# Routing half of the tokens beside the last row's scans, with scatter transfers in turn

## The chip, the cores and the metric

The kernel runs on one core of a Trainium2 chip. Its time is the device time of one execution in microseconds. The core has a matrix engine (TensorE, PE in the profile; its weight loads are shown apart as PEld), three engines that work on 128-partition tiles (VectorE or DVE, ScalarE or ACT, GpSimd or POOL), and a queue that issues plain DMA transfers (SyncE or SP). Each engine executes its own instructions in the order of its program, and waits on semaphores for others.

## The reference

Four rows (B = 4) of 1024 tokens with D = 128 columns go through two layers. The first is a state-space layer, followed by a residual and a layer norm. The second is causal attention with a residual, then a mixture of experts, a residual and a last layer norm. Cut to what matters here:

```python
# layer 1: 256 inner channels, 16 states; h is a scan along the tokens
h = scan(dA, x_scaled);  y = einsum('bldn,bln->bld', h, Cp) + xb * D_param
x = layernorm(x + out_proj(layernorm(y) * silu(z)))
# layer 2
v = ln(x) @ v_w + v_b                       # q, k likewise; 16 heads of 8
hidden = x + (softmax(causal(q k^T)) v) @ o_w + o_b
xt = layer_norm(hidden).reshape(4096, 128)
logits = xt @ router_w                      # 16 experts
top1 = argmax(logits); top2 = argmax of the rest
loc1 = cumsum(m1) - 1;  loc2 = cumsum(m2) - 1 + m1.sum(0)   # m1, m2: one-hot choices
C = 512                                     # slots of an expert, later tokens are dropped
xin[e, slot] = xt[token];  eout = fc2(gelu(fc1(xin))) * 0.8
out = layernorm(x + hidden + g1 * eout[slot1] + g2 * eout[slot2])
```

A token's slot depends on how many tokens before it chose the same expert, so ranges of tokens must be routed in order. The reference puts second choices behind all first ones; the kernel counts second choices down from the end of an expert's slots instead, so it can place them before all first choices are known, and settles at the end which of them still have a slot.

## The kernel before

**Tiles and stages.** The 4096 tokens are 32 tiles of 128. `fronts` (L263) makes projections and the convolution of the four rows, and runs beside the scans of row 0. `scan_row` (in `scans`, L358) takes a row in two halves of 512 tokens. For each pair of state groups DVE multiplies (L529), scans (L539) and multiplies by C (L545), PE sums over states (L549). POOL copies the last states of the first half (`carry`, L542). `after_scans` (L458 to L520) normalises, and twice needs an inverse root on POOL (`pow`: `ssm_rs` in L152, `lnx_rs` in L518), for which DVE waits.

**Attention** (L644 to L972) runs beside the scans of the next row: `inputs` makes q, k and v of a half (k and q go through DRAM as three bf16 parts, `k_parts` and `q_parts`, and come back as `kst` and `qst`), adds v's bias on DVE (`vp`, L714), and a stream of score matmuls (L770), exponentials on ACT (`pr`, L780) and weighted sums (L792) follows. `rest_of_half` (L844) scales the sums (`avs`, L870), projects, adds o's bias, normalises, and writes tokens to DRAM (`x2_d`, and `rest_d` for the residual); L970 keeps the router's logits in `lg`. The last half has its own version, `group_of_last` (L880), which adds o's bias from a row in a matmul (`ob_row`).

**Routing.** `routing` (L1189) makes constants. `send(t0, n)` (L1241) routes n tiles: DVE finds the first choice (`top1`), PE counts tokens ahead of each one by triangular and all-ones matmuls (`places`, L1295 and L1298), DVE turns that into a slot (`to`, `put` in L1320), then the same for the second choice. For each tile and choice an indirect DMA on POOL (`scatter`, L126) writes 128 rows of 129 numbers (the token and its own number) into `xin`. Transfers of a range are declared to hit different rows, so those of a range don't wait for each other; the first waits for those of the range before. In the first range each waits for the range's first alone.

**The order.** `piece()` (L1519) takes the next steps of several queues of work: inputs (`before`), attention, the rest of halves (`after`), weight loads, routing (`aside`) and transfers (`sending`). PE's and DVE's orders are pinned as the program is written; ACT's, POOL's and SP's come from the tile scheduler. After row 3's scans a last loop runs what is left of the attention. `send_early` (L1609) starts there: the first range is 20 tiles (40 transfers), the second 8 (16 transfers), and the last 4 tiles (8 transfers) follow the loop. Then `experts` (L1405) runs the 16 experts and combines: it loads an expert's rows (L1420), two matmuls with a gelu between (L1434, L1435, L1441), scatters back to `eout`, reads both contributions of each token (`got`), and adds (L1486) `rest_d`, which was loaded into the 32 tiles of `xrow`.

Of the kernel before, what the change touches and what calls it, by code (L numbers as in the profile page):

```python
# [10 lines left out]
F32 = mybir.dt.float32  # L11
# [26 lines left out]
NFC = F // P  # L38
EARLY = 12
# [13 lines left out]
def mamba_then_moe_block_kernel(ctx: ExitStack, tc: tile.TileContext, a: dict, out: bass.AP):  # L53
# [304 lines left out]
    def scans(ph, pools, on_loads, on_scans, on_half, spare_bank=lambda: None):  # L358
# [5 lines left out]
        s3 = ph.enter_context(tc.tile_pool(name="scan3", bufs=3))  # L364
        s6 = ph.enter_context(tc.tile_pool(name="scan6", bufs=6))
# [3 lines left out]
        a_all = wts.tile([P, DI // NR, NS], F32, tag="a_all", name="a_all")  # L369
# [16 lines left out]
        a_own = wts.tile([P, DI // NR, NG_S, NI], F32, tag="a_own", name="a_own")  # L386
# [11 lines left out]
        def half_of_scans(b, hf):  # L398
# [5 lines left out]
            def spread_states(s, ts, name):  # L404
                t = s6.tile([P, HL], F32, tag=name, name=name)
                nc.sync.dma_start(t, bc_d[b][hf][s, len(ts)].unsqueeze(0).to_broadcast([NR, NI, HL]))
                ts.append(t)
# [200 lines left out]
    def attention_weights(wts):  # L608
# [20 lines left out]
        vb = load("vb", [P, D], a["v_b"].unsqueeze(0).partition_broadcast(P), wts)  # L629
# [3 lines left out]
        wo = load("wo", [P, NG, D], a["o_w_pad"].rearrange("g p e -> p g e"), wts)  # L633
        identb = wts.tile([P, P], BF16, tag="identb", name="identb")
# [7 lines left out]
        return wq, wk, qb, kb, wv, wo, wr, vb, ob, sel_b, identb, mask_k  # L642

    def attention(ph, weights, last_bank):  # L644
# [3 lines left out]
        wq, wk, qb, kb, wv, wo, wr, vb, ob, sel_b, identb, mask_k = weights  # L648
# [7 lines left out]
        def inputs(b, hf, x1, norm, made):  # L656
# [30 lines left out]
            for n, w, bias in (("q", wq, qb), ("k", wk, kb)):  # L687
# [26 lines left out]
            nc.vector.tensor_tensor(  # L714
                vp[:, :, 0 : H * (HD + 1)].rearrange("p i (h d) -> p i h d", d=HD + 1)[:, :, :, 0:HD],
                pv.rearrange("p (i h d) -> p i h d", h=H, d=HD),
                vb.rearrange("p (h d) -> p h d", d=HD).unsqueeze(1).to_broadcast([P, 4, H, HD]), ALU.add,
# [122 lines left out]

        ob_row = load("ob_row", [1, D], a["o_b"].unsqueeze(0), p1)
# [38 lines left out]
        def group_of_last(e, g, t, rows, i0, n):  # L880
# [10 lines left out]
            if g == 0:  # L891
                e.sel = p1.tile([P, NG, 32], F32, tag="xnT", name="sel_sum")
                nc.vector.tensor_copy(
                    e.sel, ident.rearrange("p (j r) -> p j r", r=32)[:, :, HD : HD + 1].to_broadcast([P, NG, 32])
                )
                e.po = last_bank("po")
                nc.tensor.matmul(
                    e.po, lhsT=one_row, rhs=ob_row.unsqueeze(1).to_broadcast([1, TPH, D]), start=True, stop=False
                )
# [32 lines left out]
        def after_projection(e, pt, rows, i0, n, hid=None):  # L932
# [15 lines left out]
            else:  # L948
                to = rows.xrow[:, t0 : t0 + n, 0:D]
# [239 lines left out]
    def routing(ph, bank):  # L1189
# [6 lines left out]
        keep = ph.enter_context(tc.tile_pool(name="rt_keep", bufs=1))  # L1196

# [6 lines left out]
        tri_f = load("tri", [P, P], a["c_tri"], keep)  # L1204
        tri = keep.tile([P, P], BF16, tag="tri_b", name="tri_b")
        nc.vector.tensor_copy(tri, tri_f)
        ones = keep.tile([P, P], BF16, tag="ones", name="ones")
        nc.vector.memset(ones, 1.0)
        iota_i = keep.tile([P, E], I32, tag="iota_i", name="iota_i")
        nc.gpsimd.iota(iota_i, pattern=[[1, E]], base=-E, channel_multiplier=0)  # L1210
        iota_e = keep.tile([P, E], F32, tag="iota_e", name="iota_e")
        nc.vector.tensor_copy(iota_e, iota_i)
        token_i = keep.tile([P, NT], I32, tag="token_i", name="token_i")
        nc.gpsimd.iota(token_i, pattern=[[P, NT]], base=0, channel_multiplier=1)
        token = per_token("token")
        nc.vector.tensor_copy(token, token_i)
        xrow = keep.tile([P, NT, D + 1], F32, tag="xrow", name="xrow")
        nc.vector.tensor_copy(xrow[:, :, D], token)
        second = keep.tile([P, NT, E], BF16, tag="second", name="second")

        first_slot = [E * CAP - 1, E * CAP + CAP]
        alt = [per_token(f"alt{i}") for i in range(2)]
        for i in range(2):
            nc.vector.tensor_scalar(alt[i], token, float(NSLOT + i * T - first_slot[i]), None, ALU.add)
        at2, p2, place2 = per_token("at2"), per_token("p2"), per_token("place2")
        put = [keep.tile([P, NT], I32, tag=f"put{i}", name=f"put{i}") for i in range(2)]
        totals, sent = [None, None], []
        behind = keep.tile([P, E, CAP // P], F32, tag="behind", name="behind")

        def has_slot(t0, n):  # L1230

            ts = slice(t0, t0 + n)
            full = p1.tile([P, n, E], F32, tag="full", name="full")
            tt(full, second[:, ts, :], totals[0].unsqueeze(1).to_broadcast([P, n, E]), ALU.mult)
            ok = p1.tile([P, n], F32, tag="ok2", name="ok2")
            nc.vector.tensor_reduce(ok, full, AX.X, ALU.add)
            tt(ok, ok, place2[:, ts], ALU.add)
# [3 lines left out]
        def send(t0, n, later=None):  # L1241
# [3 lines left out]
            def full(name):  # L1245
                return p1.tile([P, n, E], F32, tag=name, name=name)
# [7 lines left out]
            iota_b = iota_e.unsqueeze(1).to_broadcast([P, n, E])  # L1254

            group = (f"sent{t0}", [])
            earlier = sent[-1] if sent else []
            sent.append(group[1])

            def transfers(i):  # L1260
                for t in range(t0, t0 + n):
                    ins = scatter(xin, put[i][:, t : t + 1], xrow[:, t, :], group, earlier)
                    if len(group[1]) == 1 or earlier:
                        wait_for(ins, earlier)
                    yield

            def send_rows(i):
# [3 lines left out]
                else:  # L1271
                    later(transfers(i))

# [10 lines left out]
            def places(m, i, name):  # L1284
# [5 lines left out]
                mms = [(pcum, tri, mf)]  # L1290
                mms += [(pcum[:, t * E :], ones, mf[:, 0 : (n - t) * E]) for t in range(1, n)]
# [5 lines left out]
                for t in range(n):  # L1297
                    nc.tensor.matmul(ptot, lhsT=ones, rhs=m[:, t, :], start=(t == 0), stop=(t == n - 1))  # L1298
                yield USE
                tt(loc, pcum.rearrange("p (t e) -> p t e", e=E), m, ALU.mult)  # L1300
# [10 lines left out]
            def to(i, at, place, ok):  # L1311
# [5 lines left out]
                tt(slot, slot, alt[i][:, ts], ALU.subtract)  # L1317
                tt(slot, slot, ok, ALU.mult)
                tt(slot, slot, alt[i][:, ts], ALU.add)
                nc.vector.tensor_scalar(put[i][:, ts], slot, float(first_slot[i]), None, ALU.add)  # L1320

            loc = full("loc")
# [8 lines left out]
            place1 = yield from places(m1, 0, "place1")  # L1331
# [7 lines left out]
            lg2 = full("lg2")  # L1339
            nc.vector.scalar_tensor_tensor(lg2, m1, -BIG, x, ALU.mult, ALU.add)  # L1340
            m2 = second[:, ts, :]
            mx2 = top1(lg2, m2, at2[:, ts], "mx2")
            yield
            place = yield from places(m2, 1, "place")
            nc.vector.tensor_scalar(place2[:, ts], place, -1.0, None, ALU.add)
            ok2 = has_slot(t0, n)
            to(1, at2[:, ts], place, ok2)
            send_rows(1)
            nc.vector.tensor_reduce(z, pr, AX.X, ALU.add)
            nc.vector.reciprocal(z, z)  # L1350
# [4 lines left out]
            tt(p2[:, ts], mx2, z, ALU.mult)  # L1355
            tt(gates[1][:, ts], p2[:, ts], ok2, ALU.mult)

            if later is None:
# [6 lines left out]
                    behind, pos.unsqueeze(1).to_broadcast([P, E, CAP // P]),  # L1365
                    totals[0].unsqueeze(2).to_broadcast([P, E, CAP // P]), ALU.is_ge,
                )
                nc.vector.tensor_scalar(behind, behind, float(T), None, ALU.mult)
        def all_sent(early):

            if early:
                tt(gates[1][:, 0:early], p2[:, 0:early], has_slot(0, early), ALU.mult)
# [8 lines left out]
        return xrow, send, all_sent, (behind, sent), tri_f  # L1381
# [346 lines left out]
```

## Time and profile before

| | us |
|---|---|
| runs, median of 3 | 1277.84 (1274.19 to 1285.11) |
| the profiled execution | 1291.07 |
| its span on the core | 1289.3 |
| PE busy | 937.8 (73%) |
| DVE busy | 879.9 (68%) |
| ACT busy | 673.6 (52%) |
| POOL busy | 240.3 (19%) |
| transfers into `xin`, 64 (L126) | 61.8, 965 ns each |
| mean TensorE clock granted | 0.822 of full |

The page divides the span into 40 slices of 32.2 us; each digit is an engine's busy share of a slice in tenths. Row 0 with `fronts` takes up to some 240 us, the scans of rows 1 to 3 up to about 860, the rest of the attention up to about 1100, the experts up to 1255, and the combination the rest. A timeline line has the start, the duration, the engine, the line and operation, out<-in, shapes, a count, and in brackets the idle time before it and what ended it. A waits line has who waited for whom, the total, the number of times and the longest. "remote" or "issue" there means that nothing that the profile shows released the instruction.

### The profile page before, as it was taken

How to read it: one execution, taken by the hardware profiler on the slowest of the kernel's cores; microseconds unless marked ns; L12 is line 12 of the kernel's file. 1: busy time of each engine (PE TensorE's matmuls, PEld its weight loads, DVE VectorE, ACT ScalarE, POOL GpSimd, SP SyncE). 2: the span in 40 equal slices, each digit the busy share in tenths (PEclk: the TensorE clock that was granted, in tenths of full speed). 3: DMA queues.
4: the chain of work that ended last, by engine and by line, in shares of the span. 5: the costliest groups of instructions: out<-in, count | busy, mean ns of one | idle time of the engine just before them, and what ended most of it. 6: DMA issues, size and time to landing. Idle time of an engine off the chain costs nothing. (4 is left out here: it accounts for less than half of the span.)

```text
span 1289.3 us, 15308 instructions
## 1 busy us (share of the span) xinstructions
PE 937.8 (73%) x5376; PEld 445.8 (35%) x5376; DVE 879.9 (68%) x1298; ACT 673.6 (52%) x996; POOL 240.3 (19%) x231
## 2 busy tenths in 40 slices
PE   4677851368899986889985789976428684589965
PEld 2232310035433343234332333343102232456655
DVE  2199698998999999998999998975313346122115
ACT  1467556234777784676863486834214251733324
POOL 0020111032002002012012012000650401234443
PEclk9898976567989898898987698987657696789997
DMA  3965576536535535533543440464413100712117
GB/s 71 338 218 180 183 262 224 172 98 185 180 123 185 159 110 174 155 103 120 173 134 108 142 132 10 135 146 127 139 38 101 52 11 15 203 45 66 58 35 197
DMA packets 168329, 171.02 MB, mean 133 GB/s; under 512 B 31553, under 2 KB 123154, under 8 KB 168114
## 3 DMA queue, kind: packets, MB, share of 16 engines
q1 hardware_dynamic: 152418, 142.90, 36.4%
q10 hardware_dynamic: 11728, 18.62, 4.0%
q0 software_dynamic: 4096, 8.43, 2.0%
q8 instruction: 44, 0.72, 0.2%
q14 instruction: 43, 0.35, 0.1%
HBM read 110.80 MB, written 59.10 MB: 132 GB/s over the span
## 5 line engine op out<-in xcount | busy, mean ns | idle before, releaser
L780 ACT ACTIVATE pr<-pst 128x1024 f32<-128x1024 f32 (+3 forms) x396 | 293.0, 792 | 170.2 <-PE pst L770 66.8
L533 ACT ACTIVATE da<-dt_sp,a_neg 128x512 f32<-128x512 f32 x256 | 178.7, 723 | 113.0 <-DVE h L539 101.1
L770 PE MATMUL pst<-qst,kst 72*128 72x512 bf16 (+3 forms) x792 | 199.2, 353 | 50.6 <-ACT pr L780 32.7
L792 PE MATMUL av<-pr,vp 128*32 128x512 f32 (+3 forms) x1584 | 186.9, 542 | 2.4 <-DVE pr L783 1.9
L529 DVE TENSOR_TENSOR h<-u_sp,bt 128x2048 f32<-128x2048 f32 x64 | 145.3, 2274 | 17.1 <-DMA sz_d<-sz 17.1
L539 DVE TENSOR_TENSOR_SCAN h<-da,carry,h 128x512 f32<-128x512 f32 x128 | 155.7, 1264 | 1.7 <-ACT da L533 1.7
L539 DVE TENSOR_TENSOR_SCAN h<-da,h 128x512 f32<-128x512 f32 x128 | 148.3, 1205 | 6.8 <-ACT da L533 6.8
L549 PE MATMUL py<-h,sel 128*32 128x512 f32 x512 | 87.3, 761 | 83.0 <-DVE h L545 53.5
L545 DVE TENSOR_TENSOR h<-h,ct 128x2048 f32<-128x2048 f32 x64 | 146.1, 2283 | 1.1 <-POOL carry L542 0.3
L770 PEld LDWEIGHTS <-kst 72*128 72x128 bf16 x792 | 66.2, 103 | 231.5 <-issue 211.7
L542 POOL COPY carry<-h 128x4 f32<-128x4 f32 x32 | 42.0, 1313 | 372.0 <-DVE h L539 353.3
L126 POOL DMA_INDIRECT xin<-xrow,put x64 | 61.8, 965 | 166.8 <-DVE put L1320 81.8
L1435 ACT ACTIVATE hT<-ph,b 128x512 f32<-128x512 f32 x64 | 43.8, 687 | 81.0 <-PE ph L1434 80.3
L126 POOL DMA_INDIRECT eout<-eo,to x64 | 61.3, 957 | 92.4 <-DVE eo L1446 55.4
L300 PE MATMUL pt_x<-xT,w_tap 128*128 128x512 f32 x128 | 62.8, 649 | 16.8 <-DMA xT<-in_xT_dram 7.5
L1434 PE MATMUL ph<-xeT,w 128*128 128x512 f32 x128 | 63.6, 634 | 14.8 <-DVE xeT L1430 14.8
L1441 PEld LDWEIGHTS po_e<-w,hT 128*128 128x128 f32 x512 | 61.6, 192 | 12.9 <-issue 12.0
L1441 PE MATMUL po_e<-w,hT 128*128 128x128 f32 x512 | 63.3, 276 | 0.1
L776 PE MATMUL pst<-mask_k,identb 128*128 128x128 bf16 x448 | 62.7, 224 | 0.0
L792 PEld LDWEIGHTS av<-pr,vp 128*32 128x32 f32 x1584 | 37.1, 114 | 62.4 <-issue 39.0
L549 PEld LDWEIGHTS py<-h,sel 128*32 128x32 f32 x512 | 12.5, 120 | 125.3 <-DVE h L545 65.1
L776 PEld LDWEIGHTS <-identb 128*128 128x128 bf16 x448 | 43.0, 101 | 25.7 <-issue 5.8
(247 smaller groups left out, 1148.4 us busy)
## 6 DMA issues: line engine op xcount, KB each, us to landing
dt_sp<-dt_d SPq DMA_DIRECT2D x64, 256.0 KB
u_sp<-u_d SPq DMA_DIRECT2D x64, 256.0 KB
kst<-k_parts SPq DMA_DIRECT2D x96, 144.0 KB
qst<-q_parts SPq DMA_DIRECT2D x64, 144.0 KB
bt<-bc_d SPq DMA_DIRECT2D x32, 256.0 KB
ct<-bc_d SPq DMA_DIRECT2D x32, 256.0 KB
w<-in_fc_w_dram SPq DMA_DIRECT2D x32, 256.0 KB
xin<-clear SPq DMA_DIRECT2D x8, 516.0 KB
```

The source lines that it names most:

```text
L126: ins = nc.gpsimd.indirect_dma_start(out=dst[:, :], out_offset=bass.IndirectOffsetOnAxis(ap=rows, axis=0), in_=src, in_offset=None).ins
L529: nc.vector.tensor_tensor(s.h, s.u, four(s.bt), ALU.mult)
L533: nc.scalar.activation(s.da[jl], s.dt[:, jl, :], AF.Exp, scale=a_neg[:, j, s.g : s.g + 1])
L539: ins = nc.vector.tensor_tensor_scan(h, s.da[jl], h, from_, ALU.mult, ALU.add).ins
L545: nc.vector.tensor_tensor(s.h, s.h, four(s.ct), ALU.mult)
L549: nc.tensor.matmul(s.py[jl * NR : (jl + 1) * NR, :], lhsT=sel, rhs=s.h[:, jl, :], start=(s.g == 0), stop=(s.g == NG_S - 1),)
L770: nc.tensor.matmul(pst[:, jj, :w], lhsT=ks[ki // TPH][jp][:, jj, ki % TPH * P : (ki % TPH + 1) * P], rhs=qs[jp][:, jj, q0:c1], start=True, ...
L776: nc.tensor.matmul(pst[:, jj, :P], lhsT=identb, rhs=mask_k, start=False, stop=True)
L780: nc.scalar.activation(pr[:, :, :w], pst[:, :, :w], AF.Exp, scale=QSCALE)
L792: nc.tensor.matmul(av[32 * j : 32 * j + 32, q0 : q0 + w], lhsT=e.vps[ki // TPH][:, ki % TPH, v0 : v0 + 32], rhs=pr[:, jj, :w], start=(ki = ...
L1434: nc.tensor.matmul(phh, lhsT=w1[e][:, c * P : (c + 1) * P], rhs=xeT, start=True, stop=True)
L1441: nc.tensor.matmul(po[:, i, :], lhsT=hT[:, c, i * P : (i + 1) * P], rhs=w2[e][:, c, :], start=(c == 0), stop=(c == NFC - 1),)
```

## The change

Six things change.

1. `SOON` = 16 tiles (rows 0 and 1) are a range of their own. When the fourth half is finished, during row 3's scans, `send(0, 16, ..., staged=True)` joins the queue `after`. Its transfers go out by `both_transfers`: for each tile the row is read again from `x2_d` (64 KB, SP) into one of two buffers, POOL copies the token's number in, and then both choices' transfers follow, each a step of `piece()`. The constants move to row 0 (`begin`).
2. Transfers of all ranges but the last are in turn: each waits until the one before has landed. The last range's wait for the last of those, and not for each other.
3. The tail's ranges are 8, 4 and the last 4 tiles. `xrow` has 16 tiles.
4. v's bias isn't added to v: since the weights of a token sum to one, it adds v_b @ o_w to the projection. The setup adds that to `ob`; `vp` becomes a copy on ACT, and `ob_row` with a one-row matmul becomes `ob_diag`, a diagonal matrix under an all-ones matmul.
5. Buffers: 5 instead of 6 for `bt` and `ct`, 4 instead of 5 for `got`; `a_all` and `a_own` lie in a buffer of `h`; several wide tiles of the routing share one; the residual of the first 16 tiles is loaded into its own tile (`left`).
6. The slot arithmetic of `to` takes the token and a scalar in one operation where it had a tile `alt`, and `all_sent` works in two pieces.

```diff
+SOON = 2 * TPB
...
+        once = s3.tile([P, NJ, HL], F32, tag="h", name="a_once")
+        a_all = once[:, 0, 0 : DI // NR * NS].rearrange("p (m s) -> p m s", s=NS)
...
-                t = s6.tile([P, HL], F32, tag=name, name=name)
+                t = s5.tile([P, HL], F32, tag=name, name=name)
...
+        vb = wts.tile([P, NG], F32, tag="vb", name="vb")
+        nc.gpsimd.memset(vb, 0.0)
+        for j in range(H // NG):
+            nc.sync.dma_start(
+                vb[32 * j : 32 * j + HD, :], a["v_b"].rearrange("(g j d) -> j d g", g=NG, d=HD)[j]
+            )
+        pb = bank("pb_v")
+        for g in range(NG):
+            nc.tensor.matmul(pb[:, 0:1], lhsT=wo[:, g, :], rhs=vb[:, g : g + 1], start=(g == 0), stop=(g == NG - 1))
+        nc.vector.tensor_tensor(ob, ob, pb[:, 0:1], ALU.add)
...
-            nc.vector.tensor_tensor(
+            nc.scalar.copy(
                 vp[:, :, 0 : H * (HD + 1)].rearrange("p i (h d) -> p i h d", d=HD + 1)[:, :, :, 0:HD],
                 pv.rearrange("p (i h d) -> p i h d", h=H, d=HD),
-                vb.rearrange("p (h d) -> p h d", d=HD).unsqueeze(1).to_broadcast([P, 4, H, HD]), ALU.add,
             )
...
-                    e.po, lhsT=one_row, rhs=ob_row.unsqueeze(1).to_broadcast([1, TPH, D]), start=True, stop=False
+                    e.po, lhsT=rows.ones, rhs=rows.ob_diag.unsqueeze(1).to_broadcast([P, TPH, D]), start=True, stop=False
...
-        def send(t0, n, later=None):
+        def send(t0, n, bank, later=None, staged=False):
...
-            group = (f"sent{t0}", [])
-            earlier = sent[-1] if sent else []
-            sent.append(group[1])
+            group = (f"sent{t0}", []) if later is None else None
+            earlier = in_turn[-1:]
+            if group:
+                sent.append(group[1])
+
+            def transfer(i, t, row):
+                ins = scatter(xin, s.put[i][:, t : t + 1], row, group, earlier)
+                if group:
+                    wait_for(ins, earlier)
+                else:
+                    in_turn[:] = [ins]
...
+            def both_transfers():
+
+                for t in range(t0, t0 + n):
+                    row = p2.tile([P, D + 1], F32, tag="row", name="row")
+                    nc.sync.dma_start(row[:, 0:D], x2_d[t * P : (t + 1) * P, :])
+                    nc.gpsimd.tensor_copy(row[:, D : D + 1], s.token[:, t : t + 1])
+                    yield
+                    for i in range(2):
+                        yield
+                        transfer(i, t, row)
+                        yield
...
-                tt(slot, slot, alt[i][:, ts], ALU.subtract)
+                nc.vector.scalar_tensor_tensor(slot, slot, -alt[i], s.token[:, ts], ALU.add, ALU.subtract)
                 tt(slot, slot, ok, ALU.mult)
-                tt(slot, slot, alt[i][:, ts], ALU.add)
-                nc.vector.tensor_scalar(put[i][:, ts], slot, float(first_slot[i]), None, ALU.add)
+                nc.vector.scalar_tensor_tensor(
+                    s.put[i][:, ts], slot, alt[i] + first_slot[i], s.token[:, ts], ALU.add, ALU.add
+                )
...
-        p5 = ph.enter_context(tc.tile_pool(name="moe5", bufs=5))
+        p5 = ph.enter_context(tc.tile_pool(name="moe5", bufs=4))
...
-                nc.sync.dma_start(xrow[:, :, 0:D], rest_d.rearrange("(i p) d -> p i d", p=P))
+                rest = [(xrow[:, :, 0:D], row0, NT)]
+                if row0:
+                    rest.append((p6.tile([P, row0, D], F32, tag="left", name="left"), 0, row0))
+                for t, i, j in rest:
+                    nc.sync.dma_start(t, rest_d[i * P : j * P, :].rearrange("(i p) d -> p i d", p=P))
...
-                read = (nc.scalar if k and t0 < 20 else nc.sync).dma_start(
+                read = (nc.scalar if k and t0 < 16 else nc.sync).dma_start(
...
-                                if s is aside and before or (s is loads or s is sending) and (before or middle and not pace.block):
+                                late_one = s is loads or s is sending
+                                if pace.first and ((s is aside or late_one) and before or late_one and middle and not pace.block):
                                     continue
...
                     finished.append(rest)
+                    if len(finished) * TPH == SOON:
+                        after.append(send(0, SOON, bank_z, sending.append, staged=True))
...
-                        if not aside and early < len(finished) * TPH < NT and (not early or len(finished) > 2 * B - 2):
-                            aside.append(send_early(early, len(finished) * TPH - early))
-                            early = len(finished) * TPH
+                        known = len(finished) * TPH
+                        if not aside and not before and early < known < NT and (early == SOON or known > NT - 2 * TPH):
+                            aside.append(send_early(early, known - early))
+                            early = known
                         piece()
```

## The prediction

> **What bounds the kernel now.** I read the page's slices first, then busy time by windows, then the timelines and the waits of the window that stood out.
>
> ```profile
> PE   4677851368899986889985789976428684589965
> DVE  2199698998999999998999998975313346122115
> POOL 0020111032002002012012012000650401234443
> ```
>
> One digit is 32.2 us. VectorE is at 8 or 9 from slice 7 to slice 26, so rows' scans (240 to 860 us) are bound by DVE: what is added to DVE there is paid in full. From 860 us PE leads, except in slices 28 to 30 (903 to 967 us), where no engine is busy but POOL. By windows (PE, PEld, DVE, ACT, POOL busy with instruction counts, PE clock, DMA share, GB/s):
>
> ```profile
> 780.00:840.00 60.00, 54.61 (x408) 24.10 (x406) 52.93 (x66) 45.64 (x68) 6.59 (x2) 0.97 0.25 79
> 870.00:900.00 30.00, 20.06 (x113) 10.02 (x112) 16.60 (x57) 13.18 (x20) 1.64 (x1) 0.77 0.39 118
> 930.00:960.00 30.00, 4.00 (x13) 0.69 (x13) 1.72 (x5) 2.15 (x3) 20.33 (x22) 0.50 0.15 48
> 960.00:990.00 30.00, 22.95 (x89) 8.24 (x88) 10.27 (x39) 11.72 (x16) 0.00 (x0) 0.67 0.27 81
> ```
>
> In 930 to 960 PE has 4 us of work where its neighbours have 20 to 23. It isn't bandwidth: DMA is at 0.15. What fills this window is POOL's row of transfers into `xin` (L126), 40 of them with nothing between (start, duration, then the idle time before the instruction):
>
> ```profile
> 904.79 1.20 POOL L126 DMA_INDIRECT xin<-xrow,put  x1 [32.99 <-DVE put L1320]
> 907.81 0.96 POOL L126 DMA_INDIRECT xin<-xrow,put  x1 [1.82 <-DMA xin<-xrow,put]
> 909.08 0.96 POOL L126 DMA_INDIRECT xin<-xrow,put  x1 [0.30 <-issue]
> ...
> 955.78 0.96 POOL L126 DMA_INDIRECT xin<-xrow,put  x1 [0.30 <-issue]
> ```
>
> PE in the same time:
>
> ```profile
> 916.37 1.03 PE L770 MATMUL pst<-qst,kst 72*128 72x512 bf16 x2 [4.49 <-issue]
> 933.56 0.58 PE L868 MATMUL pr<-ih,sel_b 48*128 48x512 bf16 x1 [13.10 <-DVE avs L870]
> 937.33 0.80 PE L770 MATMUL pst<-qst,kst 72*128 72x384 bf16 x2 [2.43 <-ACT pr L780]
> 961.45 0.58 PE L868 MATMUL pr<-ih,sel_b 48*128 48x512 bf16 x1 [21.45 <-DVE avs L870]
> ```
>
> 4.49 + 13.10 + 2.43 + 21.45 = 41.5 us idle, and the last gap ends 5 us after the last transfer. The engines named as releasers were waiting too:
>
> ```profile
> DVE avs L870 <- remote: 23.0, 1, 23.0
> ACT pr L780 <- remote: 22.1, 3, 15.3
> ```
>
> "remote" means that no instruction the profile shows released them: DVE's L870 had its matmul (933.56, 0.58 us) done at 934.1, was free at 937.7, and started at 960.7. In the raw events PE's semaphore rises within about 1 us of the start of the matmul that signals it in other stretches, but with a median of 4.4 us and up to 10 us late in 910 to 940, and later still after that. So what stalls PE, DVE and ACT is that PE's completions arrive late while transfers go out back to back. The second burst (16, 1005.6 to 1025.7 us) shows it smaller: PE gaps of 4.00, 1.14 and 5.25 us. Bursts of four (expert outputs) show updates at most about 1.6 us late, with one exception. The lateness grows with the length of the burst.
>
> **What the Trainium skill says.** Perfetto Trace Analysis, "DMA Instruction — SWDGE (GPSIMD)": the time shown for such a transfer is that of writing its descriptors, not of moving data. DMA: Bandwidth & Descriptors, "Anatomy of one DMA — SWDGE (gpsimd) path": about 2.0 us fixed cost, mostly the receipt of the last write. The trace agrees: the first transfer lands 2.3 to 2.7 us after its issue, and the next, which waits for it, issues at +3.02 us. So a transfer in turn costs 3.02 us, against 1.26 in a burst. SBUF — State Buffer, "Who interferes with whom": a DVE instruction with two SBUF inputs and a GpSimd one that reads SBUF exclude each other for a whole instruction. The trace agrees for ordinary POOL work:
>
> ```profile
> 732.52 0.19 POOL L542 COPY carry<-h 128x4 f32<-128x4 f32 x1 [11.95 <-DVE h L539]
> 755.90 2.17 POOL L542 COPY carry<-h 128x4 f32<-128x4 f32 x1 [7.60 <-DVE h L539]
> 788.73 2.98 POOL L152 TENSOR_TENSOR ssm_rs<-ssm_ve,neg_half 128x4 f32<-128x4 f32 x1 [30.66 <-DVE ssm_ve L150]
> 864.76 1.01 POOL L152 TENSOR_TENSOR ssm_rs<-ssm_ve,neg_half 128x4 f32<-128x4 f32 x1 [9.13 <-DVE ssm_ve L150]
> ```
>
> The same copy takes 0.19 us, or 2.17 when it starts just after a 2.26 us multiply (L529, 755.76). For transfers the trace speaks against it: in the second burst the cadence stays 1.26 to 1.27 us although L783 and L1199, with two SBUF inputs, run across transfers' starts (`full`, 1010.65 to 1010.93, over the one at 1010.87), and DVE's own starts don't slip. No page bears on PE's late semaphore.
>
> **The change part by part**, against the profiled execution (1291.07 us, of which 1289.3 span and 1.8 around it). It is 13.2 above the median of the runs, 1277.84; I take the same difference off the median, which assumes that the stalls are as long without the profiler.
>
> 1. The burst of 40 leaves the tail. 32 of its transfers go beside row 3's scans, in turn. Removed: 41.5 us of PE gaps, less some 1.5 us that PE idles in 8 us of such work anyway: -40.
> 2. The ranges left in the tail are 8 and 4 tiles, in turn (16 × 3.02 = 48 us and 8 × 3.02 = 24 us of POOL, both over well before about 1045, when the last range isn't known yet; no `pow` of POOL is in the tail). Removed: 10.4 us less about 2.4 usual idling: -8. What in-turn transfers still delay is shown only by one: the transfer at 904.79, beside which PE ran on without a gap. Bounds for 24 of them: 0, and 24 × 0.55 (the second burst's loss per transfer, 8.8 / 16) = 13. I take +3.
> 3. Routing matmuls in PE's chain: the 20-tile range has 2 × (1 + 19 + 20) of them; the first set took 907.56 to 909.5, about 2 us. A range of 8 costs about 1.1 (1007.82 to 1008.9), so 2 × 0.9, and the third range, 4 for 8, less again; with DVE's shorter operations (0.49 us at 128x320, 0.29 at 128x128) that PE's last attention steps queue behind: -4 in all (0 to -6).
> 4. Routing of 16 tiles beside the scans, on DVE: 19 wide operations; 128x256 isn't in the trace, between 0.49 and 0.29 gives 0.42, so 8.0; 20 narrow ones at 0.2, 4.0. Sum +12.0. Seven of eight `vp` adds (L714) leave DVE during scans: 0.68 us busy, next start after about 0.6, -4.2. They become copies on ACT, busy 45.6 of 60 us in 780 to 840, so hidden; if ACT were full there, they would cost 8 × about 0.7. The constants at 853.3 to 854.2 move to the setup, -1. Net +7, all on the bound engine.
> 5. POOL's and SP's queues. POOL's order after: eleven transfers stand ahead of `ssm_rs` of half (3,0), two more ahead of `lnx_rs`, all 32 ahead of the last `ssm_rs`; DVE stops for each `pow` at once (0.90 and 1.53 us at 791.7 and 798.5). First slots (`put0`) are ready at about 759, second ones at about 770 by DVE's new order. With a cadence c the eleventh transfer is out at 770 + 9c + 1, the 32nd at 770 + 30c + 1; the `pow`s are due at about 799 and, since 864.8 + 7 is when the last `ssm_ve` comes, 872. At c = 3.02 these are 798 and 862: in time. The tiny row copies and carry copies run in the 1.8 us between a transfer's end and its landing; one held by a 2.27 us multiply can overrun that by half a microsecond. At c = 3.2 to 3.3, 1 to 2 us are lost at the first `pow` and as much at the next; +4. Each row's load on SP waits for the transfers of two rows before, with `sums`, the `q_parts` stores and `kst`/`qst` loads behind it; that is the same lag, not a second one, up to 2 us of it ahead of the `kst` loads near 822. DMA is at 0.25 there: 16 × 64 KB more is nothing. Bounds: 0, and 20 at c = 4.0 (a 1 us lock wait at each transfer: 770 + 120 + 1 - 872 = 19).
> 6. The rest: bias columns and four matmuls of one column in the setup, 5 instead of 6 `bt`/`ct` buffers, the 1 MB of `left` ahead of the first expert's rows and 4 instead of 5 `got` buffers: -4 to +6, I take +2. `ob_diag` makes a 1-row matmul a 128-row one of the same columns: 0.
>
> Sum: -40 - 8 + 3 - 4 + 7 + 4 + 2 = -36. Profiled 1255; median 1277.8 - 36 = 1242.
>
> **The rivals.**
> - The stall mostly stays, or is partly the profiler's: in-turn transfers too make PE's completions late (+13 instead of +3 in part 2 and as much again in row 3), or the 13 us by which the profiled execution is longer are stall that the timed runs lack. Either gives -36 + 10 to + 25: 1252 to 1267. For it: nothing tells why bursts do this. Against: no gap beside the single transfer, and the growth with burst length.
> - Slower: POOL's in-order queue holds the `pow`s, and so DVE, behind transfers. The loss is 30c - 101; without it the sum is -40, so the change turns harmful from c = 4.7 us. If descriptors are written only between DVE's instructions, or landings come late behind 256 KB loads, c = 5.5 gives +64: 1277.8 - 40 + 64 = 1302. For it: POOL's `pow` at three times its time beside scans. Against: the uniform cadence beside L783 and L1199, and the landing wait (1.8 us) that absorbs part of each delay.
> - Between: c = 4.0, +20 instead of +4: 1258.
> - The scheduler's order could fail to send during the scans; the instruction order of the built kernel excludes it.
>
> **How the numbers follow.** Forecast (1227 to 1253) 0.62; better, under 1227, 0.05; c about 4 or a partial stall (1253 to 1276) 0.20; slower 0.13. From 1226 to 1276 all but about 2 in 10 is held. One per cent, 12.8 us, is what a measurement of this kernel can tell from no change: faster 0.79, same 0.09, slower 0.12.
>
> **What would show it.** Right: slices 28 to 30 at PE's 6 to 7, no "remote" wait of over 3 us on DVE L870's and ACT L780's successors, transfers 3.0 us apart between 759 and 870, the last row's scans ending about 7 to 12 us later. Wrong: DVE waiting long on POOL's `ssm_rs` and `lnx_rs` in row 3, transfers over 4 us apart there, or PE gaps in the tail beside transfers in turn.

## The result

The changed kernel takes 1238.95 us (median of 4 runs, 1231.83 to 1255.13); the kernel before, run beside it, 1281.47. The ratio is 0.965, 95% interval 0.9554 to 0.9747: 3.5% faster, where the forecast was 1242. Medians here are over all runs, but ratios leave out slow ones: of the changed kernel the run of 1255.13, over 1.5% above its fastest. The profiled execution is the one of 1231.83 us, with a span of 1229.9.

Slices of the page (one digit is 30.7 us):

```profile
PE   4687852267889888889988497987878873789965
DVE  2199698999899999899999999788543555112205
POOL 1020012130211001101102213454103202244443
```

The hole is gone: PE has 8, 7 and 8 in slices 28 to 30 (the first slice is 0). In the kernel before it lay in slices 28 and 29, with 4 and 2. POOL has new work in slices 24 to 27, beside row 3's scans. By windows (PE, PEld, DVE, ACT, POOL busy with counts, PE clock, DMA share, GB/s):

```profile
760.00:840.00 80.00, 64.24 (x408) 25.48 (x400) 67.60 (x70) 51.34 (x74) 39.67 (x35) 0.82 0.29 86
930.00:960.00 30.00, 25.41 (x96) 9.22 (x100) 8.43 (x34) 10.63 (x14) 9.79 (x11) 0.70 0.32 96
960.00:990.00 30.00, 25.77 (x190) 9.88 (x191) 19.57 (x58) 19.05 (x29) 7.30 (x8) 1.00 0.16 48
```

PE is busy 25 of 30 us from 930 to 960, against 4 before, with eleven transfers beside it. POOL's timeline:

```profile
755.74 0.97 POOL L127 DMA_INDIRECT xin<-row,put  x1 [8.01 <-DVE mx L1211]
...
824.07 4.06 POOL L127 DMA_INDIRECT xin<-row,put  x1 [3.37 <-issue]
...
864.09 0.96 POOL L127 DMA_INDIRECT xin<-row,put  x1 [2.65 <-issue]
869.97 0.96 POOL L127 DMA_INDIRECT xin<-row,put  x1 [4.92 <-DMA xin<-row,put]
871.36 1.05 POOL L153 TENSOR_TENSOR ssm_rs<-ssm_ve,neg_half 128x4 f32<-128x4 f32 x1 [0.43 <-DVE ssm_ve L151]
...
941.53 0.96 POOL L127 DMA_INDIRECT xin<-xrow,put  x1 [1.58 <-DMA xin<-xrow,put]
...
1036.59 0.96 POOL L127 DMA_INDIRECT xin<-xrow,put  x1 [45.30 <-DVE p L1211]
```

In the tail, after row 3's scans, most transfers start 2.55 us or little more after the one before. Beside the scans it is slower: 29 steps from 755.74 to 864.09 are 3.74 us each, and one transfer took 4.06 us of POOL instead of 0.96. The last `ssm_rs` still starts when its input is there (0.43 us on DVE, not on a transfer).

Between the two profiled executions 59.4 us went: the last `ssm_rs` is at 871.4 instead of 864.8 (+6.6); from there to the first transfer of the last range it is 165.2 us instead of 225.8 (-60.6); from there to the end 193.3 instead of 198.7 (-5.4). Row 3 alone takes 19.5 us longer, 191.8 instead of 172.3; the changed execution was 12.9 us ahead when that row began, which nothing here explains.

### The profile page after: what moved, and what is told of

Read it like the earlier page. It is cut to its first block, busy times and chain, and to the rows that moved or that the text cites. A ratio compares the mean times of both kernels' runs of the same rounds, so it can differ in the third digit from the quotient of the medians.

```text
span 1229.9 us, 15466 instructions
## 1 busy us (share of the span) xinstructions
PE 923.8 (75%) x5388; PEld 442.2 (36%) x5388; DVE 880.8 (72%) x1328; ACT 678.4 (55%) x1006; POOL 265.2 (22%) x248
## 5 line engine op out<-in xcount | busy, mean ns | idle before, releaser
L536 ACT ACTIVATE da<-dt_sp,a_neg 128x512 f32<-128x512 f32 x256 | 179.0, 722 | 117.9 <-DVE h L542 106.8
L804 PE MATMUL av<-pr,vp 128*32 128x512 f32 (+3 forms) x1584 | 181.3, 526 | 2.0 <-DVE pr L795 1.6
L532 DVE TENSOR_TENSOR h<-u_sp,bt 128x2048 f32<-128x2048 f32 x64 | 145.4, 2276 | 16.5 <-DMA u_sp<-u_d 16.5
L782 PEld LDWEIGHTS <-kst 72*128 72x128 bf16 x792 | 66.3, 103 | 183.0 <-issue 153.5
L545 POOL COPY carry<-h 128x4 f32<-128x4 f32 x32 | 44.6, 1392 | 355.6 <-DVE h L542 336.9
L1476 PE MATMUL ph<-xeT,w 128*128 128x512 f32 x128 | 61.9, 619 | 12.9 <-DVE xeT L1472 12.9
L127 POOL DMA_INDIRECT xin<-row,put x32 | 47.0, 1468 | 77.1 <-issue 29.3
L127 POOL DMA_INDIRECT xin<-xrow,put x32 | 31.1, 971 | 137.5 <-DVE p L1211 45.3
```

The costliest lines, as they stand in the source:

```text
L127: ins = nc.gpsimd.indirect_dma_start(out=dst[:, :], out_offset=bass.IndirectOffsetOnAxis(ap=rows, axis=0), in_=src, in_offset=None).ins
L532: nc.vector.tensor_tensor(s.h, s.u, four(s.bt), ALU.mult)
L536: nc.scalar.activation(s.da[jl], s.dt[:, jl, :], AF.Exp, scale=a_neg[:, j, s.g : s.g + 1])
L782: nc.tensor.matmul(pst[:, jj, :w], lhsT=ks[ki // TPH][jp][:, jj, ki % TPH * P : (ki % TPH + 1) * P], rhs=qs[jp][:, jj, q0:c1], start=True, ...
L804: nc.tensor.matmul(av[32 * j : 32 * j + 32, q0 : q0 + w], lhsT=e.vps[ki // TPH][:, ki % TPH, v0 : v0 + 32], rhs=pr[:, jj, :w], start=(ki = ...
L1476: nc.tensor.matmul(phh, lhsT=w1[e][:, c * P : (c + 1) * P], rhs=xeT, start=True, stop=True)
```

## The experiments

They were run in sets, each on one chip with runs of the kernel before beside it; ratios are to those. The theory (T): transfers sent back to back make completions reach the engines late, and the gain comes from ending that. The rival (P, place): it comes from moving routing and transfers out of the tail.

| set, kernel before | kernel | median us | ratio (95% interval) |
|---|---|---|---|
| first, 1281.47 | the changed kernel | 1238.95 | 0.965 (0.9554 to 0.9747) |
| second, 1284.1 | before_turn | 1268.66 | 0.9881 (0.9854 to 0.9907) |
| | before_two | 1242.27 | 0.9702 (0.9629 to 0.9774) |
| | before_spaced | 1271.32 | 0.9912 (0.988 to 0.9944) |
| | after_tail_burst | 1256.8 | 0.9795 (0.9762 to 0.9827) |
| third, 1283.15 | after_soon0 | 1272.58 | 0.9907 (0.9877 to 0.9936) |
| | after_v_on_dve | 1247.84 | 0.969 (0.9637 to 0.9742) |
| | after_two | 1243.9 | 0.962 (0.9552 to 0.9688) |
| | soon0_two | 1246.63 | 0.9699 (0.9647 to 0.975) |
| fourth, 1231.7 | after_again | 1247.51 | 1.0108 (1.006 to 1.0155) |
| | after_last_two | 1239.74 | 1.0091 (1.0062 to 1.0119) |
| | spaced_write | 1238.79 | 1.0059 (1.0038 to 1.0079) |
| fifth, 1282.59 | soon0_burst | 1281.37 | 0.9985 (0.9963 to 1.0007) |

### Transfers in turn alone

```diff
-            group = (f"sent{t0}", [])
-            earlier = sent[-1] if sent else []
-            sent.append(group[1])
+            group = (f"sent{t0}", []) if later is None else None
+            earlier = in_turn[-1:]
+            if group:
+                sent.append(group[1])
...
-                    if len(group[1]) == 1 or earlier:
-                        wait_for(ins, earlier)
+                    if group:
+                        wait_for(ins, earlier)
+                    else:
+                        in_turn[:] = [ins]
```

> The kernel before with one edit: the transfers of the first two ranges (40 and 16) wait each for the landing of the one before; routing and transfers stay in the tail. Theory (transfers sent back to back make the semaphores of all engines late): the PE gaps beside the first two ranges go, 42 + 8 us, a little of it given back since POOL needs 102 us for 40 transfers, so 35 to 50 us faster than before (ratio 0.962 to 0.973). Rival (the gain of the change comes from moving routing and transfers out of the tail): within 1% of before.

Only 15 us faster, neither of the two. The gaps did go: windows, PE's timeline and waits of before_turn:

```profile
930.00:960.00 30.00, 26.45 (x149) 9.83 (x142) 14.08 (x45) 11.50 (x17) 9.57 (x10) 0.73 0.24 70
```

```profile
1027.60 0.27 PE L1301 MATMUL pcum<-second,ones 128*128 128x16 bf16 x4
1079.63 1.11 PE L1431 MATMUL pt_xe<-ident,xe 128*128 128x128 f32 x4 [51.75 <-DMA xe<-xin]
```

```profile
POOL xin L126 <- DMA xin<-xrow,put: 111.6, 56, 4.7
DVE to_f L1426 <- DMA xe<-xin: 57.9, 6, 47.2
```

PE ends the attention at 1027.6, some 60 us before it did. From the last `ssm_rs` to the end of the last routing matmul, in the kernel before, in before_turn and in the changed kernel:

```profile
864.76:1091.21 226.45, 135.80 (x819) 58.10 (x817) 88.61 (x298) 71.15 (x110) 57.38 (x59) 0.70 0.23 72
861.90:1027.87 165.97, 125.65 (x819) 54.82 (x817) 88.90 (x298) 70.63 (x110) 43.53 (x45) 0.80 0.30 92
871.36:1037.43 166.07, 127.77 (x759) 52.34 (x757) 82.12 (x291) 70.77 (x111) 26.93 (x27) 0.77 0.31 92
```

With all of the routing still in it, before_turn's stage is as short as the changed kernel's. So P doesn't explain this gain. But after it PE stands still for 51.75 us (13.9 in the kernel before) until the first expert's rows are there. 56 transfers in turn occupy POOL's queue for 165 us (899.8 to 1065.3), longer than what is left of the attention. So waiting for each landing ends the stall, and in its place POOL sets the end. The expectation missed this although it had the 102 us of the first range; the second range stood behind it.

### At most two under way

```diff
-            first = [] if earlier else group[1][:1]
+            first = ([] if earlier else group[1][:1]) + (group[1][-2:][:1] if dst is xin and len(group[1]) >= 2 else [])
```

> The kernel before with one edit: a transfer of the first two ranges waits for the landing of the one two before it, so that at most two are under way; with 2.3 us to landing the cadence stays near 1.3 us. If the number under way makes semaphores late: 35 to 50 us faster, as with transfers in turn. If the rate of transfers does it: at most 10 us faster, and the PE gaps stay. Rival of the place: within 1%.

38 us faster, as the expectation has it for the number under way. Neither the routing nor the 56 transfers left the tail: P falls here too as the reason of the whole gain. The window of before_two:

```profile
930.00:960.00 30.00, 25.24 (x95) 8.45 (x96) 12.39 (x39) 12.14 (x14) 17.68 (x18) 0.60 0.44 137
```

POOL is nearly as busy there as in the kernel before, and PE works. Both ranges are out by 994. But the number isn't set apart from the rate by this: the wait also makes pauses, 40 transfers take 67 us instead of 52, and beside a stretch at 1.3 us (973 to 980) PE's completions were up to 2.5 us late again. Nor is all of the stall gone: from the last `ssm_rs` to the last routing matmul it is 185.8 us, 20 more than in before_turn. before_two is faster than before_turn since PE then waits 14.5 us for the first expert's rows, not 51.75.

### Spaced by work of POOL

```diff
+                    if later is not None:
+                        nc.gpsimd.tensor_copy(filler, put[i][:, t : t + 1].to_broadcast([P, 1000]))
```

> The kernel before with one edit: behind each transfer of the first two ranges POOL copies 1000 integers per partition (about 1 us), no wait for landings added. The cadence becomes 2.3 to 2.8 us. If the rate does it: 30 to 50 us faster. If it takes the wait for a landing to keep semaphores in time: at most 10 us faster.

Only 11 us faster, but not because the stall stayed: at a cadence of about 2.2 us and with no wait for landings, PE's completions were at most 1.7 us late once that cadence was reached. DVE paid instead:

```profile
967.37 2.25 DVE L783 TENSOR_TENSOR pr<-pr,tri 128x256 f32<-128x256 f32 x2
973.96 2.25 DVE L783 TENSOR_TENSOR pr<-pr,tri 128x256 f32<-128x256 f32 x2
```

Two of these take 0.75 us in the kernel before; beside POOL's copies of 1.02 us they take 2.25. It is the exclusion of the Trainium skill's SBUF — State Buffer ("Who interferes with whom"), by which a DVE instruction with two SBUF inputs and a GpSimd one that reads SBUF can't run together; here it is DVE that waits. From the last `ssm_rs` to the last routing matmul DVE is busy 133 us instead of 89. So a slower rate ends most of the lateness too, and the kernel's time says nothing on T. The repeat with a filler that mostly writes was to settle it:

```diff
-                        nc.gpsimd.tensor_copy(filler, put[i][:, t : t + 1].to_broadcast([P, 1000]))
+                        nc.gpsimd.tensor_copy(filler[:, 0:1], put[i][:, t : t + 1])
+                        nc.gpsimd.memset(filler, 0)
```

> before_spaced with another filler: between transfers of the first two ranges POOL in turn copies one number per partition and fills 1000 (a write alone, which should not hold up DVE's instructions with two SBUF inputs); no landing waits. If the rate is what makes semaphores late, and before_spaced lost its gain to DVE waiting for POOL's copies: 25 to 42 us faster than before, DVE's L783 and L1199 at their usual 0.38 and 0.29 us. If a landing wait is needed: at most 12 us faster, with PE gaps as before.

It came into the fourth set, in which the kernel before seems to have no stall (below), so it settles nothing on T. It does show that this filler leaves L783 alone: 0.43 us each and 0.47 at most, against 0.79 and 1.92 in before_spaced. Others it holds up: L195, with one wide SBUF input, takes up to 1.71 us instead of 0.35.

### Bursts put back into the changed kernel's tail

```diff
-            group = (f"sent{t0}", []) if later is None else None
-            earlier = in_turn[-1:]
+            group = None if staged else (f"sent{t0}", [])
+            earlier = sent[-1] if sent else in_turn[-1:]
```

> The changed kernel with one edit: the ranges of 8 and 4 tiles in the tail go out back to back, as before the change; the 32 transfers beside the scans stay in turn. Theory: PE gaps as beside the second burst of the kernel before, 0.5 to 0.6 us for each of 24 transfers, so 8 to 14 us slower than the changed kernel. Rival of the place: within 4 us of the changed kernel.

1.5% over the changed kernel's ratio, some 18 us (the intervals of the two ratios leave 2 to 35). PE gaps of 4.68 and 4.10 us beside the bursts are there again. In the traces 12.7 us of the difference lie ahead of the bursts (the last `ssm_rs` at 884.1), most of it one wait that the changed kernel has in some executions too (part 5 below), and from there to the last range it is 180.7 us instead of 165.2: 15.5 us for 24 transfers, a little more than expected.

### Nothing beside the scans

```diff
-SOON = 2 * TPB
+SOON = 0
```

> The changed kernel with SOON = 0: nothing is routed beside the scans, the first range is 20 tiles in the tail, transfers in turn; v's bias stays behind the projection. If transfers in turn need the POOL time beside the scans (before_turn: 56 of them took 165 us of POOL and the first expert waited for them): near before_turn less the 4 us of vp adds, 1258 to 1268, so 20 to 28 us slower than the changed kernel, with a wait of 40 us and more for the first expert's rows. If the staging is worth nothing: within 6 us of the changed kernel.

Of the expected kind, and 5 us over the expected range: 1272.58, bound by POOL like before_turn, with PE waiting 62.9 us for the first expert's rows. With transfers in turn the staging, which is routing 16 tiles beside row 3's scans, is worth 2.6%. With two under way, which is this edit in the kernels soon0_two (SOON = 0) and after_two (SOON as in the change), it is worth nothing that can be told:

```diff
-            first = [] if earlier else group[1][:1]
+            first = ([] if earlier else group[1][:1]) + (group[1][-2:][:1] if group[0] == "early" else [])
...
-            earlier = in_turn[-1:]
+            earlier = in_turn[-2:]
...
-                ins = scatter(xin, s.put[i][:, t : t + 1], row, group, earlier)
+                ins = scatter(xin, s.put[i][:, t : t + 1], row, group or ("early", in_turn), earlier if group else ())
                 if group:
                     wait_for(ins, earlier)
-                else:
-                    in_turn[:] = [ins]
```

> after_soon0 with at most two transfers under way: nothing beside the scans, DVE free of 12 us of routing there, v's copies on ACT. From before_two (1242) less 4 us for v: 1234 to 1242, so within 5 us of the changed kernel, and 20 us and more faster than after_soon0. If staging gains by more than it avoids POOL's backlog: 8 us and more slower than the changed kernel.

> The changed kernel with one edit: transfers of all ranges but the last wait for the landing of the one two before, not one before. If landing waits cost nothing after the change since POOL has the time: within 4 us of the changed kernel. If POOL's queue still holds SP's row loads and the stores behind them beside the scans: 4 to 10 us faster.

0.9699 (soon0_two), 0.962 (after_two) and 0.965 (the change) overlap in their intervals; neither expectation can be told from its rival. As in before_two, part of the stall is left: 188.4 us from the last `ssm_rs` to the last routing matmul in soon0_two, against 163.1 in after_soon0. The staging is one way to give POOL its time; two under way is another.

### v's copies on DVE

```diff
-            nc.scalar.copy(
+            nc.vector.tensor_copy(
```

> The changed kernel with the eight copies of v on DVE in place of ACT (no bias is added there, it stays behind the projection). The prediction's 0.6 us for each of seven in the scans: 3 to 6 us slower than the changed kernel, row 3's last normalisation 4 us later. If DVE has slack there after all: within 1.5 us.

0.969 against 0.965, with overlapping intervals: undecided. Each copy takes 0.68 us on DVE, as the add did, but the runs don't resolve seven of them.

### The same kernel once more

> The changed kernel once more, beside others on the same chip. Ratio to before 0.960 to 0.970 expected.

A plain miss. In this set the kernel before took 1231.7 us, the changed one 1247.51: 1.1% slower. The changed kernel is 0.7% above its first median, but the kernel before is 50 us faster than in the other sets, as if it had no stall. There is no trace of it in this set, so this isn't shown directly. The three traces that are there send no long bursts, but show no late completions either: in all of after_again PE's and DVE's completions come within 0.05 us of the end of their instruction, beside the last eight transfers and the experts' groups of four as well, which go out back to back (0.06 and 0.35 us at most in the other two). In the changed kernel of the first set they are up to 3.6 us late beside such groups. The tail of spaced_write, with the routing and 56 transfers in it, takes 183.5 us from the last `ssm_rs` to the last range, against 225.8 in the kernel before with its stall, although the filler keeps DVE busy there for 104 us instead of 89.

Making the last eight wait too changes nothing that can be told there (1.0091):

> The changed kernel with one edit: every transfer into xin, the last eight too, waits for the landing of the one two before it. In the changed kernel DVE's semaphores are up to 10 us late in the last eight, but the first expert waits for the landings anyway. If that lateness costs nothing: within 4 us of the changed kernel. If it holds the first expert: 4 to 8 us faster.

The last run asked again, with the routing in the tail and bursts in place:

> The changed kernel with SOON = 0 and bursts as before the change: of the change only v's bias, the buffers and the shorter slot arithmetic are left, the first burst has 40 transfers again. In the last comparison the kernel before took 1232 us where it had taken 1284 on other chips, and all recorded completions were in time; so whether a burst stalls the engines may differ from chip to chip. On a chip where the kernel before takes about 1284: 0 to 8 us faster than it, PE gaps of 40 us beside the 40 transfers. On one where it takes about 1232: 2 to 10 us faster (v's adds off DVE), PE with no gap over 6 us beside the 40 transfers, and no completion over 0.1 us late. If instead the first burst never stalls this kernel: 1225 to 1240 on any chip.

In its set the kernel before took 1282.59 again, and the stall is in the trace (PE's timeline of soon0_burst, the transfers from 898.9 on):

```profile
924.10 0.58 PE L878 MATMUL pr<-ih,sel_b 48*128 48x512 bf16 x1 [8.41 <-issue]
943.07 3.78 PE L886 MATMUL po<-avs,wo 128*128 128x512 f32 x4 [15.98 <-DVE avs L880]
970.45 1.11 PE L937 MATMUL pt_po<-ident,poT 128*128 128x128 f32 x4 [14.75 <-ACT poT L933]
```

The fourth and the fifth set bear the same chip's number, so the number doesn't decide it. What decides whether a burst stalls stays open: in four sets of five it does, in one it seems not to. One difference is in the traces themselves: in sets with the stall 8 to 47 of some 1500 completions of PE are missing from the record, in the fourth set none (before_turn, whose tail has no stall, lacks 8 too). Whether the recording of events is itself what is held up was not tried: every run here comes with a span and a granted clock, as such a recording gives them, and none shows the kernel without it. For the lateness told in the prediction this means that some of it may be a lost record, after which the next one was taken; PE's idle time doesn't depend on that.

No kernel of these beats both the kernel before and the changed one in every set. before_two and after_two are level with the change where there is a stall; before_two wasn't run in the fourth set.

## Why the prediction was right

The main step was right: where transfers no longer go out back to back, the stall goes. That the sum came out as well is in part luck. The tail gained about 11 us more than forecast, row 3 cost about 9 more, and in the fourth set, which seems to lack the stall, the same change is a loss. By stages, in the traces (the tail from row 3's last `ssm_rs` to the end of the last routing matmul, then the wait until PE has the first expert's rows):

| us | rows 0 to 2 | row 3 | tail | wait | the rest |
|---|---|---|---|---|---|
| before | 692.4 | 172.3 | 226.4 | 13.9 | 184.1 |
| soon0_burst | 686.2 | 170.8 | 227.7 | 13.4 | 187.3 |
| before_turn | 684.6 | 177.3 | 166.0 | 51.8 | 187.3 |
| after_soon0 | 688.3 | 171.0 | 163.1 | 62.9 | 187.1 |
| before_two | 683.8 | 175.5 | 185.8 | 14.5 | 183.0 |
| soon0_two | 686.3 | 171.4 | 188.4 | 14.1 | 189.0 |
| the changed kernel | 679.5 | 191.8 | 166.1 | 13.5 | 179.0 |
| after_two | 685.6 | 188.7 | 172.1 | 13.3 | 182.0 |
| after_again | 685.0 | 205.6 | 165.5 | 13.2 | 179.3 |

- **Parts 1 and 2, the stall (-48, with +3 left), and part 3, routing out of the tail (-4).** Together they forecast -49 for the tail; it was -60. before_turn and after_soon0, with transfers in turn and all routing in the tail, are as short there (163 to 166 us) as the staged kernels (162 to 172). So the stall was worth about 60, and taking the routing out of the tail nothing that the traces can tell; -4 is within their scatter. Nor did attention move: 172 of its 792 score matmuls lie in the tail of the kernel before and of the changed one alike. Of before_turn's 60, PE's idle time is 50 (90.7 us before, 40.3 then), about what the gaps added up to. The other 10 are the part that the prediction didn't count: the same matmuls kept PE busy for 135.8 us with the stall and 125.7 without, at a mean granted clock of 0.70 and 0.80. That the clock is all of it isn't shown. Beside transfers in turn nothing is left: in before_turn's tail PE's completions are at most 0.5 us late.
- **Part 4, DVE beside the scans (+12 for routing).** From `ssm_rs` of row 2's end to that of row 3's, DVE is busy 162.6 us in the changed kernel and 152.3 in soon0_burst: +10.3. The 128x256 operation takes 0.42 us, as interpolated. The gain from v (-4.2) isn't resolved: soon0_burst, which has it with the new buffers and slot arithmetic, is 1.2 us under the kernel before by medians, -4.7 to +0.9 by its interval.
- **Part 5, the queues (+4). This is the step that failed**, and the price of the whole staging with it. Counted from row 2's last `ssm_rs`, the first two transfers went out when forecast (after 65.9 and 76.2 us; forecast 66.6 and 77.6). The cadence was 3.74 instead of 3.2 to 3.3 us, and still DVE's waits for `ssm_rs` and `lnx_rs` in the middle of row 3 were 2.6 and 2.7 us, only 2.9 over those of before: the row had become longer, so the last `ssm_rs` came due later than forecast (191.8 us after row 2's, not 180). Row 3 takes 189 to 206 us in six staged kernels and 171 to 177 in eight others: about +25 (+19.5 in the changed kernel's own trace) where parts 4 and 5 had +16 between them. DVE's work is 10 of it. The rest is idle time of DVE: 18.7 us in soon0_burst, 29.3 in the changed kernel, 43 in after_again. SP's waits in the changed kernel and in after_again, and a stretch of after_again, show one cause:

```profile
SPq L1295 <- DMA xin<-row,put: 53.7, 12, 7.7
```

```profile
SPq L1295 <- DMA xin<-row,put: 69.4, 13, 9.8
```

```profile
836.77 10.65 SPq L1295 DMA_DIRECT2D row<-x_d  x2
837.43 0.56 ACT L843 COPY avs<-av 128x512 f32<-128x512 f32 x1
849.66 0.55 SPq L847 DMA_DIRECT2D sums<-avs  x1
855.51 0.55 DVE L863 RECIPROCAL rd<-rd 128x64 f32<-128x64 f32 x1 [8.39 <-DMA rd<-sums]
```

  Row loads (L1295) hold SP for up to 9.8 us each, waiting for transfers. `sums` was ready to be stored at 838.0; behind two row loads and the `qst` and `kst` loads it was issued at 849.66, and DVE stood still for 8.39 us until it had come back. The prediction called that "the same lag, not a second one"; it is a second one. This wait of 8.1 to 8.6 us is in three staged traces (after_again, after_tail_burst, after_v_on_dve), whose row 3 takes 202 to 206 us; in the other three it is 1.5 us at most, and row 3 takes 189 to 192. What is left of the 25 is in waits of a few us each and isn't traced to a cause.
- **The reading that transfers don't wait for DVE** failed. Beside the scans the 32 transfers took 1.47 us on average against 0.96 (4.06 us at most, 5.28 in after_again). Of the 14 that took over 1.15 us in the changed kernel, 13 end 0.77 to 0.84 us after a scan or a multiply of DVE ended, as if each had waited for it. The evidence for it was a stretch with operations of 0.3 to 0.4 us, too short to hold a transfer visibly; the carry copies of 0.19 and 2.17 us, which the prediction showed, were the better guide. The other half of it held: DVE's multiply (L532) takes 2278 ns beside transfers, 2273 before.
- **Part 6 (+2)**: from the first expert's rows on, the six staged traces take 179 to 182 us, the kernel before and its variants 183 to 187: some -4, and why isn't shown.
- **Small slips of reading.** DVE's 8s and 9s end with slice 25; slice 26 has 7. PE's hole is slices 28 and 29 (903 to 967 us); slice 30 has 8. Part 2 takes 8 us for the second burst's loss, and its bound 8.8 for the same loss. None of these moves the sum.

By stages, -60 + 25 - 4 with some -2 in rows 0 to 2 is about -41, against a measured -42.5 by medians (-45 by the ratio, 32 to 57 faster) and a forecast of -36. Without the stall, the prediction's other terms sum to +9 (-4 + 7 + 4 + 2); the fourth set shows +13 (1.08% of 1231.7, 7 to 19). That agrees with the sum, though not with its terms.

The rival of a stall that is only partly there had two reasons. That transfers in turn stall PE too is refuted by before_turn. That the 13 us by which the profiled execution is longer are stall is unlikely: it reached the end of row 2, ahead of all transfers, at 692.4 us, and the four variants with the same scans at 681.3 to 686.9, so 6 to 11 of the 13 had been lost by then. What the fourth set suggests instead is a stall that is there or isn't, and this no rival had.

## What to carry to other kernels

When every engine stands still beside one engine's queue, and the named releaser had long been done, ask what that queue is doing at that rate: here, limiting the transfers under way to two gave the same total as the whole change with one line, and waiting for each of them ended the stall but moved the wait to POOL until POOL was given other time. Compare stages and not only totals: before_two and after_two have nearly equal totals here, and lose their time in different stages. Work put beside a bound stage costs its instructions and also every in-order queue that it stands in: loads that wait for a slow queue hold up the stores behind them. Measure the kernel before on more than one occasion: a stall that belongs to the circumstances makes a change look better than it is.

## What the runs showed of the hardware

- Indirect transfers sent every 1.26 us can hold up completions of PE and DVE: by the record up to 10 us for PE in the kernel before and 16 in soon0_burst, with PE standing still for up to 21.45 us at a time. A stage with 56 of them took 226 us instead of the 166 that it takes when each waits for the landing of the one before (2.96 us from one to the next on average in before_turn, 2.55 at best). At most two under way (1.7 us on average) left some 20 of these 60 us; at a spacing of about 2.2 us without a wait PE's completions were at most 1.7 us late. In one set of runs of five the stall seems not to have occurred at all, and whether it occurs without the recording is open.
- An indirect transfer beside row 3's scans, with their long DVE instructions, takes 0.96 to 5.28 us of POOL; those over 1.15 us end 0.77 to 0.84 us after a DVE instruction did, in 13 cases of 14. It doesn't slow DVE's multiply (2278 ns beside transfers, 2273 without). A POOL copy of 1000 integers that reads SBUF does slow DVE: a pair of multiplies goes from 0.75 to 2.25 us. One that fills as many without reading leaves such multiplies at 0.43 us each.
